# Group statistics in three steps between units, and a first look one block ahead, in a four-layer vision kernel

## The chip, the cores and the metric

The kernel runs on one core of one Trainium2 chip. The time is the device time of one execution in microseconds, as the median of several runs of the same program. The core has five engines, each with an instruction queue of its own: TensorE (PE in the profile, and PEld for its weight loads), VectorE (DVE), ScalarE (ACT), GpSimd (POOL) and SyncE (SP), which here issues most of the data transfers. They wait for one another through semaphores.

## The reference

The input is a batch of 4 images of 56 x 56 positions with 256 channels, in float32. Four residual layers follow one another, each behind a group normalisation without weights:

```python
def _gn(v, G=32, eps=1e-5):
    g = v.reshape(B_, H_, W_, G, C_ // G)
    m = jnp.mean(g, axis=(1, 2, 4), keepdims=True)
    s = jnp.var(g, axis=(1, 2, 4), keepdims=True)
    return ((g - m) / jnp.sqrt(s + eps)).reshape(v.shape)

x = x + L0(_gn(x))   # 7x7 neighbourhood attention, 8 heads, zero padding
x = x + L1(_gn(x))   # all 3136 tokens of an image against each other
x = x + L2(_gn(x))   # 7x7 neighbourhood attention in two halves of the heads, dilation 1 and 2
x = x + L3(_gn(x))   # 7x7 windows shifted by 3, 8 heads, relative position bias
```

Layers 0, 2 and 3 project to queries, keys and values, take softmax(q k + bias) v in the neighbourhood or window, and project the result. Layer 1 normalises each token to unit length, forms exp(5(A - max A)) of A = xn W_adj xn without its diagonal, scales its rows to sum 1, and passes rowsum * (xW + b) - A xW through a layer norm and a leaky ReLU. What matters here is that the mean and the variance of a group of 8 channels run over the whole image: nothing of an image can be normalised in a layer before the last part of that image has left the layer before it.

## The kernel before

`direct_blocks` holds all four layers, one after the other, each over the images 0 to 3. Between layers an image lies in DRAM as channels by tokens. On chip the 256 channels are two halves (`CC` = 2) of 128 partitions.

**Statistics.** `add_stats(l, b, i, x)` (L888) takes `bn_stats` of part i of image b as soon as that part of the input of layer l is on chip: for layer 0 from loads of their own (`first_look`, L1096), for layers 1 to 3 from the output of the layer before (L1220, L1413, L1599). `group_stats(l, b, pm)` (L894) is called when the image is first to be normalised. It puts out, in one go,

- two `bn_aggr` on DVE, which make mean and variance of each channel (`mv`, L901);
- a 128x2 matmul with the matrix `group`, which averages over the 8 channels of a group (L902), and its copy to `gst` (L903);
- three DVE operations on 128x2, which make (channel mean - group mean)^2 + variance (`dv`, L905 to L907);
- a second matmul with `group` over `dv` (L908), eps added on DVE (L909), and the power -0.5 on GpSimd (L910), with a second GpSimd operation that records the numbers (L912).

`normalise` (L914) then applies (x - mean) * scale to a half of a tile on DVE (L915, result `xn`). Both small matmuls take a PSUM buffer with the tag "m" (`ps_m`), of which there are two in layers 0, 2 and 3 and one in layer 1. The same two buffers take every projection: `project` (L917, matmul L921; keys, queries, output) and `value_rows` (L932, matmul L938; values), so that a third projection in a row waits until the first is taken out of PSUM. Keys and queries are taken out by ScalarE, values and the output projection of layers 0 and 2 by DVE.

**Units and steps.** Layers 0 and 2 work on a stream of pairs of tiles (`attend_pairs`, L1006): per pair the scores (PE, L1019), a bias (DVE, L1026) and two exponentials (ACT, L1027 and L1029), two multiplications by table or mask on GpSimd (L1030, L1039), and the products with the values (PE, L1048). TensorE runs the scores of a pair, then `w["fill"]`, then the products of the pair before, so that what lies in the fill covers the time of the exponentials. A unit is 7 rows of an image in layer 0 (8 units per image, 4 pairs each) and 14 rows in layer 2 (4 per image, 8 pairs each). The steps of a unit (projections of a later block, `prepare`, the output projection of the unit before, the building of a table for a later layer) stand in one list, and `spread` (L1068) divides that list evenly by its length over the unit's pairs. Layer 3 does the same by half rows of windows (`attend_quads`, L957), with its list written out for each.

**Layer 0.** Unit r takes `steps` from the rows of projections, puts `project_out(r - 1)` in the middle, and in the first four units of an image loads two parts each of the next image under the tag "xs" (three buffers) and takes their first look; the fourth unit ends with `group_stats(0, b + 1)`. **Layer 1** has the units (image, tile, range of tiles); `tokens(b, c)` normalises 512 tokens, makes their norms (`sq`, L1294; L1299) and projects them, and calls `group_stats(1, b)` for c = 0 (L1287). The accumulation of the products is on DVE (`acc`, L1359). **Layers 2 and 3** call `group_stats` in `prepare`, for the first part of an image (L1473, L1722), about one unit ahead of its use.

In layers 0 to 2 the order of instructions on each engine is set by a scheduler that goes by the order of the program and by priorities; in layer 3 it is the order of the program (`manual_schedule`).

Of the kernel before, what the change touches and what calls it, by code (L numbers as in the profile page):

```python
# [24 lines left out]
FP = mybir.dt.float32  # L25
# [6 lines left out]
NIMG = 4  # L32
# [799 lines left out]
def direct_blocks(ctx: ExitStack, tc: tile.TileContext, d: dict, watch):  # L832
# [38 lines left out]
    def psum_tile(tag, bufs, banks=1):  # L871
        shape = [P, 512] if banks == 1 else [P, banks, 512]
        return ps.tile(shape, FP, tag=tag, name="ps_" + tag, bufs=bufs)

    def ps_m():
        return psum_tile("m", 2)

    def weight(pool, name, n):
        w = pool.tile([P, CC, n], FP, name="w_" + name)
# [3 lines left out]

    parts_of = [NCH, NB0, NCH, 2 * NSB]
    raw = [[const.tile([P, CC, n, 6], FP, name=f"st{l}_{b}") for b in range(NIMG)] for l, n in enumerate(parts_of)]
    stats = {}

    def add_stats(l, b, i, x):  # L888

        if l < 4:  # L890
            for h in range(CC):
                nc.vector.bn_stats(out=raw[l][b][:, h, i, :], in_=x[:, h, :])

    def group_stats(l, b, pm):  # L894

        st = raw[l][b]
        mv = const.tile([P, CC, 2], FP, name=f"mv{l}_{b}")
        gst = stats[l, b] = const.tile([P, CC, 2], FP, name=f"gst{l}_{b}")
        dv = const.tile([P, CC], FP, name=f"dv{l}_{b}")
        for h in range(CC):  # L900
            nc.vector.bn_aggr(out=mv[:, h, :], in_=st[:, h].rearrange("p a b -> p (a b)"))  # L901
        nc.tensor.matmul(pm[:, :CC], lhsT=group, rhs=mv[:, :, 0], start=True, stop=True)  # L902
        nc.vector.tensor_copy(gst[:, :, 0], pm[:, :CC])  # L903

        nc.vector.tensor_tensor(dv, mv[:, :, 0], gst[:, :, 0], ALU.subtract)  # L905
        nc.vector.tensor_tensor(dv, dv, dv, ALU.mult)
        nc.vector.tensor_tensor(dv, dv, mv[:, :, 1], ALU.add)  # L907
        nc.tensor.matmul(pm[:, CC:2 * CC], lhsT=group, rhs=dv, start=True, stop=True)  # L908
        nc.vector.tensor_scalar_add(dv, pm[:, CC:2 * CC], GN_EPS)  # L909
        nc.gpsimd.tensor_tensor(gst[:, :, 1], dv, mhalf, ALU.pow)  # L910
        w = watch[1][:, :2 * CC].rearrange("p (h a) -> p h a", h=CC)
        nc.gpsimd.tensor_tensor(w, w, gst, ALU.add)  # L912

    def normalise(dst, src, gst, h):  # L914
        nc.vector.tensor_scalar(dst, src, gst[:, h, 0:1], gst[:, h, 1:2], ALU.subtract, ALU.mult)  # L915
# [171 lines left out]
    def layer0(big, pool):  # L1087
# [2 lines left out]

        def load(r, held=xs, tag="x"):
            b, g = divmod(r, NCH)
            held[r] = pool.tile([P, CC, CH], FP, tag=tag, name="x0", bufs=3)
            nc.sync.dma_start(out=held[r], in_=tokens_of(0, b, g * CH, CH))

        def first_look(r):  # L1096
# [3 lines left out]
        for r in (3, 4, 5, 6, 0, 1, 2):  # L1100
# [2 lines left out]
                add_stats(0, 0, r, xs[r])  # L1103
            else:
                first_look(r)
        group_stats(0, 0, ps_m())
        wv, wk, wq = (weight(big, n, C) for n in ("wv0", "wk0", "wq0"))
        late_loads()
        wo = weight(big, "wo0", C)
# [10 lines left out]
        def prepare(r):  # L1120
            xn = xns[r] = pool.tile([P, CC, CH], FP, tag="xn", name="xn0")
            x = xs.pop(r)
            for h in range(CC):
                normalise(xn[:, h, :], x[:, h, :], stats[0, r // NCH], h)
            if 3 < r + 2 < NIMG * NCH:
                load(r + 2)

# [96 lines left out]
        def stream():  # L1224
            n = NIMG * NCH
            rows = []
            for c in range(2, n):
                rows += lazily(project_rows, c, 6)
                rows.append(lambda c=c: prepare(c + 1) if c + 1 < n else None)
            gone = 0  # L1230
            for r in range(NIMG * NB0):
                b, g = divmod(r, NB0)
                to = min(len(rows), (7 * (7 * r + 12)) // 8)
                steps, gone = rows[gone:to], to
                if r:
                    at = len(steps) // 2
                    steps[at:at] = project_out(r - 1)
                if b + 1 < NIMG and g < 4:
                    for i in range((b + 1) * NCH + 2 * g, (b + 1) * NCH + min(2 * g + 2, NCH)):
                        load(i, looks, "xs")  # L1240
                        steps.append(lambda i=i: first_look(i))
                    if g == 3:
                        steps.append(lambda b=b: group_stats(0, b + 1, ps_m()))
                if r:
                    steps += table[:3]
                    del table[:3]
                attns[r] = pool.tile([P, CC, BT], FP, tag="attn", name="attn0")
                yield from spread([pair(r, t) for t in range(NTC)], steps)

# [18 lines left out]
    def layer1(big, pool):  # L1268
        NB = -(-T // P)
        real = lambda i: min(P, T - i * P)  # L1270
        ps_a = lambda: psum_tile("m", 1)
        w_aff = weight(big, "waff", C)
        xnT = big.tile([P, CC, NB * P], FP, name="xnT")
        xw = big.tile([P, NB, C + 1], FP, name="xw")
# [7 lines left out]
        def tokens(b, c):  # L1282

            tiles = range(4 * c, min(4 * c + 4, NB))
            n = sum(real(t) for t in tiles)
            if c == 0:
                group_stats(1, b, ps_a())  # L1287
            x = pool.tile([P, CC, 512], FP, tag="x", name="x1")
            nc.sync.dma_start(out=x[:, :, :n], in_=tokens_of(1, b, 4 * c * P, n))
            x1 = pool.tile([P, CC, 512], FP, tag="xn", name="xn1")  # L1290
            sq = pool.tile([P, CC, 512], FP, tag="sq", name="sq")
            for h in range(CC):
                normalise(x1[:, h, :n], x[:, h, :n], stats[1, b], h)
            nc.scalar.activation(sq[:, :, :n], x1[:, :, :n], AF.Square)  # L1294
            k = real(tiles[0])
            pm = ps_a()
# [127 lines left out]
        for k, w in enumerate(units):  # L1424
            b, j, first, last = w
            while waiting and waiting[0][0] <= done:
                waiting.pop(0)[1]()
            if j == 0:
                c = first // 4 + 2 if b == 0 else NC4 - 1 if first == 0 else NC4
                if c < NC4:  # L1430
                    tokens(b, c)
            if first == j:
                residual(b, j * P // CH)
                residual(b, j * P // CH + 1)
                if j % 4 == 2 and j >= 6 and b + 1 < NIMG:
# [14 lines left out]


    def layer2(big, pool):
        (types1, w1), (types2, w2) = window_types(S), window_types(G2)
        w_qkv, w_p = weight(big, "wqkv2", 3 * C), weight(big, "wp2", C)
        bias = big.tile([P, 4, w1 + w2], FP, name="bias2")
# [13 lines left out]

        def prepare(i):  # L1470
            b, c = divmod(i, 2 * NSB)
            if c == 0:
                group_stats(2, b, ps_m())  # L1473
            x = xs.pop(i)
            if i + 1 < NIMG * 2 * NSB:
                load(i + 1)
            xn = xns[i] = pool.tile([P, CC, WC2], FP, tag="xn", name="xn2")
            for h in range(CC):
                normalise(xn[:, h, :], x[:, h, :], stats[2, b], h)

        def project_rows(i):

# [120 lines left out]
        def stream():  # L1603
            n = NIMG * NSB
            for r in range(n):
                steps = []
                for i in (2 * r + 3, 2 * r + 4):
                    if i < 2 * n:
                        steps += lazily(project_rows, i, 6)
                    if i + 1 < 2 * n:  # L1610
                        steps.append(lambda i=i: prepare(i + 1))
                if r:
                    at = max(1, len(steps) // 4)
                    steps = steps or [no_step]
                    steps[at:at] = project_out(r - 1)
                attns[r] = pool.tile([P, CC, 2 * WC2], FP, tag="attn", name="attn2")
                yield from spread([pair(r, m, i) for i in range(4) for m in range(2)], steps)

# [73 lines left out]
    def layer3(big, pool):  # L1692
# [25 lines left out]
            transfer(3, r, xs[r], 0)  # L1718

        def prepare(r):  # L1720
            if r % 8 == 0:
                group_stats(3, r // 8, ps_m())  # L1722
            x = xs.pop(r)
            if r + 1 < NIMG * 8:
                load(r + 1)
            xn = xns[r] = pool.tile([P, CC, WC], FP, tag="xn", name="xn3")
            for h in range(CC):
                for w, xv in parts(xn[:, h, :], x[:, h, :]):
                    normalise(w, xv, stats[3, r // 8], h)

        def project_rows(r):
            xn = xns.pop(r)
# [59 lines left out]
        def stream():  # L1792
            n = NIMG * 8
            for r in range(n):
                attns[r] = pool.tile([P, CC, WC], FP, tag="attn", name="attn3", bufs=3)
                rows = lazily(project_rows, r + 1, 6) if r + 1 < n else []
                out = project_out(r - 2) if r > 1 else []
                for hq in range(CC):
                    steps = out[hq:hq + 1] + rows[3 * hq:3 * hq + 3]
                    if hq and r + 2 < n:  # L1800
                        steps.append(lambda r=r: prepare(r + 2))
                    w = quad(r, hq)
                    w["fill"] = lambda steps=steps: [f() for f in steps]
                    yield w
# [121 lines left out]
```

## Time and profile before

| | before |
|---|---|
| time, median of 3 runs | 4215.47 us (4213.47 to 4218.94) |
| span of the profiled execution | 4208.6 us |
| layer 0 / 1 / 2 / 3, from the trace | 0-807 / 807-2903 / 2903-3624 / 3624-4208 us |
| busy: TensorE, its weight loads | 3983.2, 2790.2 us |
| busy: DVE, ACT, POOL | 2375.0, 1348.8, 1739.3 us |
| sets of group statistics | 16 (4 layers x 4 images), two small matmuls each |

In the profile a busy figure counts the time in which at least one instruction of that engine was under way. Idle time is put down to the instruction that ended it ("waited for"). An entry such as "128x2 f32 x16" gives partitions, elements and count. Some rows carry the line of a helper: L921 is every projection, whichever layer it is in. The granted clock (PEclk) is the share of TensorE's full clock that the chip allowed in that stretch.

### The profile page before, as it was taken

Reading aid. Unit: us, or ns where it says so; the run is one execution under the profiler, and the core shown is the slowest. Engines: PE = TensorE matmul, PEld = TensorE weight load, DVE = VectorE, ACT = ScalarE, POOL = GpSimd, SP = SyncE. Lnnn points to the kernel's source line nnn. Section 1 sums busy time; section 2 is a strip of 40 time slices with the busy share of each in tenths; the row PEclk is TensorE's granted clock in tenths of the full one; section 3 lists DMA queues with packets and bytes.
Section 4 is the critical chain, followed back from the end, with each engine's and each line's share of the span. In section 5 each row is a group of like instructions: output and inputs, shape, how many; then the busy total and the mean of one; then the engine's idle time right before and its main releaser. Section 6 shows DMA issues by size and latency. Waiting matters only on the chain.

```text
span 4208.6 us, 92416 instructions
## 1 busy us (share of the span) xinstructions
PE 3983.2 (95%) x39191; PEld 2790.2 (66%) x39191; DVE 2375.0 (56%) x4437; ACT 1348.8 (32%) x2850; POOL 1739.3 (41%) x1883
## 2 busy tenths in 40 slices
PE   7899999799999999999999999996999999799998
PEld 4566666577777677776777677774666666566665
DVE  6777777533445333453434533344677878566665
ACT  3345545321211112211112111111545555334333
POOL 2466667511124111241112411123766767444444
PEclk9899999899999999999999999998999999899999
DMA  7343333300000000010000000003343433322222
GB/s 254 94 124 118 117 110 107 100 16 9 24 14 28 19 10 24 15 37 10 14 19 24 18 9 9 10 18 119 108 124 116 126 112 117 104 71 71 71 71 64
DMA packets 239793, 275.88 MB, mean 66 GB/s; under 512 B 22150, under 2 KB 231720, under 8 KB 238888
## 3 DMA queue, kind: packets, MB, share of 16 engines
q1 hardware_dynamic: 239082, 269.80, 20.9%
q8 instruction: 310, 5.08, 0.5%
q14 instruction: 113, 0.93, 0.1%
q10 hardware_dynamic: 288, 0.08, 0.0%
HBM read 190.29 MB, written 79.53 MB: 64 GB/s over the span
## 4 chain that ended last, share of the span: by engine, by line
PE 81%; DVE 8%; POOL 5%; issue 2%; DMA 2%; ACT 1%; SPq 0%; DVEq 0%; POOLq 0%; ACTq 0%
PE ps_m L921 17%; PE ps_o L1363 13%; PE ps_v L1355 11%; PE ps_s L1335 11%; PE ps_m L938 8%; PE ps_o L1048 6%; PE ps_s L1019 5%; PE ps_t L1350 3%; PE ps_o L988 2%; POOL b L1039 1%; PE ps_s L973 1%; PE ps_m L1309 1%; PE ps_m L1299 1%; DMA x<-x 1%; POOL rstd L1393 1%
## 5 line engine op out<-in xcount | busy, mean ns | idle before, releaser
L1359 DVE TENSOR_TENSOR acc<-acc,ps_v 128x257 f32<-128x257 f32 x1104 | 459.0, 420 | 677.2 <-PE ps_v L1355 673.0
L1338 ACT ACTIVATE e<-ps_s 128x512 f32<-128x512 f32 (+3 forms) x364 | 200.7, 551 | 1418.3 <-PE ps_s L1335 1418.0
L1355 PE MATMUL ps_v<-xw,e 128*128 128x257 f32 x2400 | 639.9, 384 | 13.6 <-DVE acc L1359 13.6
L1363 PE MATMUL ps_o<-xw,at 128*128 128x257 f32 x2400 | 642.6, 390 | 0.3
L1335 PE MATMUL ps_s<-xnT,xd 128*128 128x512 f32 (+3 forms) x1456 | 631.1, 550 | 0.0
L1363 PEld LDWEIGHTS ps_o<-xw,at 128*128 128x128 f32 x2400 | 436.7, 190 | 128.6 <-ACT at L930 70.7
L1039 POOL TENSOR_TENSOR b<-e 126x336 f32<-126x336 f32 (+5 forms) x512 | 501.2, 1001 | 11.2 <-ACT e L1027 3.1
L1355 PEld LDWEIGHTS ps_v<-xw,e 128*128 128x128 f32 x2400 | 423.1, 191 | 93.5 <-DVE acc L1359 33.8
L1331 POOL TENSOR_SCALAR xd<-xnT,vec 128x128 f32<-128x128 f32 x200 | 121.9, 621 | 812.4 <-PE ps_s L1335 807.1
L921 PE MATMUL ps_m<-xn,w_wqkv 128*128 128x392 f32 x1024 | 370.8, 502 | 16.0 <-DVE xn L915 15.8
L1335 PEld LDWEIGHTS ps_s<-xnT,xd 128*128 128x128 f32 x1456 | 264.1, 190 | 141.2 <-issue 117.2
L1030 POOL TENSOR_TENSOR e<-e,m0t 126x672 f32<-126x672 f32 (+3 forms) x128 | 238.7, 1865 | 270.7 <-ACT e L1029 270.7
L1030 POOL TENSOR_TENSOR e<-e,bias 119x784 f32<-119x784 f32 (+5 forms) x128 | 239.8, 1873 | 223.0 <-ACT e L1029 222.9
L951 ACT ACTIVATE no<-rs 128x168 f32<-128x168 f32 (+2 forms) x256 | 93.8, 367 | 625.4 <-DVE rs L1562 288.9
L921 PEld LDWEIGHTS ps_m<-xn,w_wqkv 128*128 128x128 f32 x1024 | 188.6, 191 | 150.3 <-ACT pr L1785 17.2
L938 PE MATMUL ps_m<-w_wqkv,xn 128*98 128x256 f32 x1024 | 246.8, 390 | 19.9 <-DVE xn L915 19.9
L1048 PEld LDWEIGHTS ps_o<-e,vp 124*32 124x32 f32 (+3 forms) x8192 | 174.0, 110 | 135.9 <-issue 76.8
L915 DVE TENSOR_SCALAR xn<-x,gst 128x28 f32<-128x28 f32 (+4 forms) x368 | 202.2, 604 | 95.9 <-PE ps_m L921 50.5
L1350 PEld LDWEIGHTS ps_t<-ident,e 128*128 128x128 f32 x1200 | 152.2, 142 | 143.0 <-issue 136.4
L1048 PE MATMUL ps_o<-e,vp 124*32 124x112 f32 (+3 forms) x8192 | 235.4, 252 | 4.0 <-POOL e L1030 3.4
L1562 DVE RECIPROCAL rs<-ps_o 128x196 f32<-128x196 f32 (+2 forms) x128 | 176.4, 1378 | 99.6 <-PE ps_o L1048 97.0
L940 DVE TENSOR_TENSOR v<-ps_m,bc 98x512 f32<-98x512 f32 (+1 forms) x184 | 125.4, 687 | 188.2 <-PE ps_m L938 111.4
(149 smaller groups left out, 6260.3 us busy)
## 6 DMA issues: line engine op xcount, KB each, us to landing
x<-xr SPq DMA_DIRECT2D x64, 392.0 KB
x<-in_x SPq DMA_DIRECT2D x53, 448.0 KB
x<-x SPq DMA_DIRECT2D x60, 392.0 KB
xr<-x SPq DMA_DIRECT2D x60, 392.0 KB
vd<-v SPq DMA_DIRECT2D x28, 448.0 KB
xr<-in_x SPq DMA_DIRECT2D x32, 392.0 KB
xr<-x SPq DMA_DIRECT2D x28, 448.0 KB
x<-xr SPq DMA_DIRECT2D x28, 448.0 KB
```

The lines of the kernel that those rows point to most:

```text
L915: nc.vector.tensor_scalar(dst, src, gst[:, h, 0:1], gst[:, h, 1:2], ALU.subtract, ALU.mult)
L921: nc.tensor.matmul(pm[:, :n], lhsT=w[:, h, col:col + P], rhs=rhs(h), start=(h == 0), stop=(h == CC - 1))
L938: nc.tensor.matmul(pm[:n, j * C:(j + 1) * C], lhsT=xn[:, h, k * n:(k + 1) * n], rhs=w[:, h, :], start=(h == 0), stop=(h == CC - 1))
L1019: nc.tensor.matmul(s[j // 2][:nk, j % 2, (2 * i + u) * nq:(2 * i + u + 1) * nq], lhsT=k(j, u), rhs=q(j), start=True, stop=True)
L1030: nc.gpsimd.tensor_tensor(parts(ev), parts(ev), w["emask"], ALU.mult)
L1039: nc.gpsimd.tensor_tensor(w["b"][a][:nk, :, :2 * nq].rearrange("p h (i c) -> p h i c", i=2), ev[:, :, :, 0, :], ev[:, :, :, 1, :], ALU.add)
L1048: nc.tensor.matmul(w["o"](k, i)[j * HD:(j + 1) * HD], lhsT=ones[:nk, :HD] if k else v(j, u), rhs=w["b"][j // 2][:nk, j % 2, i * nq:(i + 1) ...
L1335: nc.tensor.matmul(s[:, :n], lhsT=xd[j][:, h, :], rhs=xnT[:, h, first * P:last * P], start=(h == 0), stop=(h == CC - 1))
L1350: nc.tensor.transpose(pt[:, col(i)], e[:, col(i)], ident)
L1355: nc.tensor.matmul(pv[:, :C + 1], lhsT=e[:, col(i)], rhs=xw[:, j, :], start=True, stop=True)
L1359: nc.vector.tensor_tensor(acc[:, i, :], acc[:, i, :], pv[:, :C + 1], ALU.add)
L1363: nc.tensor.matmul(out[j][:, :C + 1], lhsT=e[:, col(i)] if i == j else at[:, col(i)], rhs=xw[:, i, :], start=(i == j), stop=(i == NB - 1))
```

## The change

The statistics of an image are no longer computed where they are first needed but as soon as the last part of the image is known, and in three steps that can stand apart: `channels` (the two `bn_aggr`), `mean` (the first matmul to `dv`) and `scale` (the second matmul to the power). `add_stats` counts the parts, and the last one puts the three steps into `pending`. `step_stats` does one of them, if there is one, and stands in the lists of steps: in layer 0 three times in the first unit of an image and in the last four, in layer 1 at every fourth unit, in layer 2 three times in every unit from the second on, in layer 3 at the end of each half row. `known(l, b)` takes the place of `stats[l, b]` and does whatever is left. So that steps which are left over may run in the next layer, `ps_m` takes its number of buffers from `m_bufs`, and each layer sets it as it was.

In layer 0 the parts for the first look are loaded one unit ahead of the look (`look_at`), into four buffers instead of three, and the looks come first in a unit's list. `project_out` goes in last, so that its place in the middle is reckoned in the longer list.

```diff
     def add_stats(l, b, i, x):
         if l < 4:
             for h in range(CC):
                 nc.vector.bn_stats(out=raw[l][b][:, h, i, :], in_=x[:, h, :])
-    def group_stats(l, b, pm):
+            seen_parts[l, b] = seen_parts.get((l, b), 0) + 1
+            if seen_parts[l, b] == parts_of[l]:
+                pending.extend(group_stats(l, b))
+
+    def group_stats(l, b):
...
+        def channels():
...
+        def mean():
+            pm = ps_m()
...
+        def scale():
+            pm = ps_m()
...
+            stats[l, b] = gst
+        return [channels, mean, scale]
+
+    def step_stats():
+        if pending:
+            pending.pop(0)()
+
+    def known(l, b):
+        while (l, b) not in stats:
+            pending.pop(0)()
+        return stats[l, b]
...
-            held[r] = pool.tile([P, CC, CH], FP, tag=tag, name="x0", bufs=3)
+            held[r] = pool.tile([P, CC, CH], FP, tag=tag, name="x0", bufs=3 if tag == "x" else 4)
...
+            look_at = {}
+            for b in range(NIMG - 1):
+                for i in range(NCH):
+                    look_at.setdefault(NB0 * b + min(i // 2 + (b == 0), 3), []).append((b + 1) * NCH + i)
             for r in range(NIMG * NB0):
...
-                if r:
-                    at = len(steps) // 2
-                    steps[at:at] = project_out(r - 1)
-                if b + 1 < NIMG and g < 4:
-                    for i in range((b + 1) * NCH + 2 * g, (b + 1) * NCH + min(2 * g + 2, NCH)):
-                        load(i, looks, "xs")
-                        steps.append(lambda i=i: first_look(i))
-                    if g == 3:
-                        steps.append(lambda b=b: group_stats(0, b + 1, ps_m()))
+                steps += [lambda i=i: first_look(i) for i in sorted(looks)]
+                steps.append(lambda r=r: [load(i, looks, "xs") for i in look_at.get(r + 1, [])])
+                for i in range(3 if g > 3 or g == 0 else 0):
+                    steps.insert(2 * i, step_stats)
                 if r:
                     steps += table[:3]
                     del table[:3]
+                    at = (len(steps) + 1) // 2
+                    steps[at:at] = project_out(r - 1)
...
         def tokens(b, c):
-            if c == 0:
-                group_stats(1, b, ps_a())
...
         for k, w in enumerate(units):
+            if k % 4 == 2:
+                step_stats()
...
@@ layer 2, prepare and stream @@
-            if c == 0:
-                group_stats(2, b, ps_m())
...
                     steps[at:at] = project_out(r - 1)
+                    for _ in range(3):
+                        at = min(at + 5, len(steps))
+                        steps.insert(at, step_stats)
...
@@ layer 3, prepare and stream @@
-            if r % 8 == 0:
-                group_stats(3, r // 8, ps_m())
...
                         steps.append(lambda r=r: prepare(r + 2))
+                    steps.append(step_stats)
```

Every normalisation reads `known(l, b)` instead of `stats[l, b]`.

More of the change, by code (lines that the diff above doesn't have):

```diff
@@ L873, in psum_tile @@
         return ps.tile(shape, FP, tag=tag, name="ps_" + tag, bufs=bufs)
+    m_bufs = 2
     def ps_m():
-        return psum_tile("m", 2)
+        return psum_tile("m", m_bufs)
     def weight(pool, name, n):
@@ L885, in direct_blocks @@
     raw = [[const.tile([P, CC, n, 6], FP, name=f"st{l}_{b}") for b in range(NIMG)] for l, n in enumerate(parts_of)]
-    stats = {}
+    stats, pending = {}, []
+    seen_parts = {}
     def add_stats(l, b, i, x):
@@ L892, in add_stats @@
                 nc.vector.bn_stats(out=raw[l][b][:, h, i, :], in_=x[:, h, :])
-    def group_stats(l, b, pm):
+            seen_parts[l, b] = seen_parts.get((l, b), 0) + 1
+            if seen_parts[l, b] == parts_of[l]:
+                pending.extend(group_stats(l, b))
+    def group_stats(l, b):
         st = raw[l][b]
         mv = const.tile([P, CC, 2], FP, name=f"mv{l}_{b}")
-        gst = stats[l, b] = const.tile([P, CC, 2], FP, name=f"gst{l}_{b}")
+        gst = const.tile([P, CC, 2], FP, name=f"gst{l}_{b}")
@@ L899, in group_stats @@
         dv = const.tile([P, CC], FP, name=f"dv{l}_{b}")
[L900 to L912, printed above, removed]
+        def channels():
+            for h in range(CC):
+                nc.vector.bn_aggr(out=mv[:, h, :], in_=st[:, h].rearrange("p a b -> p (a b)"))
+        def mean():
+            pm = ps_m()
+            nc.tensor.matmul(pm[:, :CC], lhsT=group, rhs=mv[:, :, 0], start=True, stop=True)
+            nc.vector.tensor_copy(gst[:, :, 0], pm[:, :CC])
+            nc.vector.tensor_tensor(dv, mv[:, :, 0], gst[:, :, 0], ALU.subtract)
+            nc.vector.tensor_tensor(dv, dv, dv, ALU.mult)
+            nc.vector.tensor_tensor(dv, dv, mv[:, :, 1], ALU.add)
@@ new lines, in scale @@
+        def scale():
+            pm = ps_m()
+            nc.tensor.matmul(pm[:, :CC], lhsT=group, rhs=dv, start=True, stop=True)
+            nc.vector.tensor_scalar_add(dv, pm[:, :CC], GN_EPS)
+            nc.gpsimd.tensor_tensor(gst[:, :, 1], dv, mhalf, ALU.pow)
+            w = watch[1][:, :2 * CC].rearrange("p (h a) -> p h a", h=CC)
+            nc.gpsimd.tensor_tensor(w, w, gst, ALU.add)
+            stats[l, b] = gst
[3 more added lines that the diff above has]
+            pending.pop(0)()
@@ L1105, in layer0 @@
                 first_look(r)
-        group_stats(0, 0, ps_m())
+        known(0, 0)
         wv, wk, wq = (weight(big, n, C) for n in ("wv0", "wk0", "wq0"))
@@ L1123, in prepare @@
             for h in range(CC):
-                normalise(xn[:, h, :], x[:, h, :], stats[0, r // NCH], h)
+                normalise(xn[:, h, :], x[:, h, :], known(0, r // NCH), h)
             if 3 < r + 2 < NIMG * NCH:
@@ L1270, in layer1 @@
         real = lambda i: min(P, T - i * P)
-        ps_a = lambda: psum_tile("m", 1)
+        nonlocal m_bufs
+        m_bufs, ps_a = 1, ps_m
         w_aff = weight(big, "waff", C)
@@ L1292, in tokens @@
             for h in range(CC):
-                normalise(x1[:, h, :n], x[:, h, :n], stats[1, b], h)
+                normalise(x1[:, h, :n], x[:, h, :n], known(1, b), h)
             nc.scalar.activation(sq[:, :, :n], x1[:, :, :n], AF.Square)
@@ L1452, in layer2 @@
     def layer2(big, pool):
+        nonlocal m_bufs
+        m_bufs = 2
         (types1, w1), (types2, w2) = window_types(S), window_types(G2)
@@ L1478, in prepare @@
             for h in range(CC):
-                normalise(xn[:, h, :], x[:, h, :], stats[2, b], h)
+                normalise(xn[:, h, :], x[:, h, :], known(2, b), h)
         def project_rows(i):
@@ L1728, in prepare @@
                 for w, xv in parts(xn[:, h, :], x[:, h, :]):
-                    normalise(w, xv, stats[3, r // 8], h)
+                    normalise(w, xv, known(3, r // 8), h)
         def project_rows(r):
```

## The prediction

> **What bounds the kernel now.** I read the page's busy times and slices first, then the waits of TensorE, then the timeline of one place where group statistics are computed, then equal stretches of time beside each other for their cost.
>
> ```profile
> span 4208.6 us, 92416 instructions
> PE 3983.2 (95%) x39191; PEld 2790.2 (66%) x39191; DVE 2375.0 (56%) x4437; ACT 1348.8 (32%) x2850; POOL 1739.3 (41%) x1883
> PEclk9899999899999999999999999998999999899999
> ```
>
> TensorE is busy 95% of the span and nothing else is over 56%. So the time is TensorE's work, plus its idle 225 us (4208.6 - 3983.2), plus what it loses where its granted clock is below 1. An edit that leaves the work alone, as this one does, can only win from the last two. The waits of TensorE, as "who waited <- for what: us in total, times, longest":
>
> ```profile
> PE ps_m L908 <- DVE dv L907: 28.7, 13, 3.8
> ...
> PE ps_m L902 <- DVE mv L901: 18.6, 4, 14.5
> ...
> PE ps_m L921 <- ACT no L951: 14.2, 7, 2.7
> PE ps_v L1355 <- DVE acc L1359: 13.6, 43, 1.6
> PE ps_m L921 <- DVE attn L1194: 10.7, 6, 2.7
> PE ps_m L921 <- ACT kE L1145: 10.6, 6, 3.8
> ```
>
> L902 and L908 are the two matmuls of the statistics, L921 a projection. The 14.5 us of L902 is the program's start. The rest of L908 is what the change aims at. One such place, in layer 2 (columns: start, duration, engine, line, operation; the bracket is the idle time before):
>
> ```profile
> 3053.69 0.28 PE L902 MATMUL ps_m<-mv,group 128*128 128x2 f32 x2
> 3053.90 0.86 PE L1048 MATMUL ps_o<-e,vp 119*32 119x98 f32 x26
> 3053.97 2.09 POOL L1030 TENSOR_TENSOR e<-e,bias 124x896 f32<-124x896 f32 x1 [2.54 <-ACT e L1029]
> ...
> 3054.20 1.87 DVE L905 TENSOR_TENSOR dv<-mv,gst 128x2 f32<-128x2 f32 x1
> ...
> 3056.02 2.21 POOL L1039 TENSOR_TENSOR b<-e 124x448 f32<-124x448 f32 x2
> 3056.11 1.05 DVE L906 TENSOR_TENSOR dv<-dv 128x2 f32<-128x2 f32 x1
> 3057.20 1.05 DVE L907 TENSOR_TENSOR dv<-dv,mv 128x2 f32<-128x2 f32 x1
> ...
> 3058.30 0.38 PE L908 MATMUL ps_m<-dv,group 128*128 128x2 f32 x2 [3.54 <-DVE dv L907]
> ```
>
> Three operations on 128x2 take 1.87, 1.05 and 1.05 us; each ends as one of GpSimd's ends, and where GpSimd is still they take 0.10 to 0.16. TensorE has 26 attention matmuls to do meanwhile (0.86 us) and then sits for 3.54 us behind the second matmul, although the attention matmuls queued after it need nothing from it. The idle time is not all: the same attention work before, after and behind the gap (columns: window, sum; busy PE, PEld, DVE, ACT, POOL; granted clock, DMA share, GB/s):
>
> ```profile
> 3013.00:3019.00 6.00, 6.00 (x109) 4.64 (x100) 5.97 (x7) 2.50 (x6) 4.42 (x4) 1.00 0.57 161
> 3059.50:3068.40 8.90, 8.90 (x106) 6.54 (x100) 6.89 (x9) 2.03 (x4) 3.94 (x5) 0.67 0.42 121
> 3104.00:3110.00 6.00, 6.00 (x116) 4.65 (x114) 5.47 (x7) 2.41 (x5) 5.51 (x5) 1.00 0.58 163
> ```
>
> The clock falls to 0.67 on average, and 106 matmul records take 8.9 us where 109 take 6.0: the gap costs almost as much again afterwards.
>
> [...]clock records at 0.5 follow the statistics gaps and last 3.41 us or twice that.[...] So what decides a wait is how much of TensorE's own work stands between the two small matmuls.[...]
>
> **The change, part by part.** Every engine keeps its instructions; only the order moves. I take the cost of an episode from equal stretches: what a unit with statistics takes over its neighbours, less 0.55 us for the four small matmul records that stay (0.28 + 0.38, less what overlaps).
>
> Layer 3: a half row takes 8.25 us (distance of successive ones in the timeline); the three with statistics, at 3759, 3895 and 4032, take 4.55, 4.55 and 6.41 more, although the idle gaps there are only 1.35 at L902 and 0.83 at L908; the rest is half clock. Sum 15.5, less 3 x 0.55 = **13.9 us**. In the changed order these sets are computed in layer 2, with their two matmuls two pairs (some 10 us) apart, so no wait is left; I take 14.
>
> Layer 2: a unit takes 41.3 us; with statistics 49.0, 47.3 and 48.9, sum 21.3, less 1.6 = **19.7 us**. These sets move into layer 1, which has one episode less of its own. Against it: the three statistics steps that are inserted into a unit's list, nearly all of them empty, shift all later steps over the pairs, in every unit from the second on. A projection needs one of two PSUM buffers of tag m, so a third in one pair must wait until the first is emptied. Before, 13 units have such a pair, "output, key, key", whose first buffer DVE empties in about 0.6 us; weight loads wait on DVE's L1597 there for 4.1 us in all, 0.3 each. After, that pair is gone, and 13 units have "key, output, output" in one pair and "key, key, query" in another, whose first buffer ScalarE empties. In a pair of before (3085) the key projection starts at 3084.98 and the second projection ends at 3087.9; ScalarE empties the keys, behind two exponentials of 0.80 and 0.86 us, from 3087.77 to 3088.89. A third one would so have waited 1.0 us there. ScalarE's place varies by some 0.6 us: between 0.4 and 1.0, and I take 0.7. 26 x 0.7 = 18 us given back, less the 4 of the pair that went: 14. Bounds: 26 x 0.4 - 4 = 6 and, by the waits of layer 0 on L1145 without the longest, (10.6 - 3.8)/5 = 1.36, 26 x 1.36 - 4 = 31. Layer 2: 19.7 - 14 = **+6**.
>
> Layer 0: three episodes cost 5.7, 7.6 and 7.0 over neighbouring units, 20.3 less 1.6 = 18.7. Afterwards the first matmul and the second lie a pair apart in four places, with attention (1.26), scores (1.13) and a value projection (1.6 to 1.9) between them: 4.0 to 4.3 us of work against 4.1 us of the three DVE operations at their slowest; that hides them but for some 0.2. In two further places (pairs 12.3 and 20.3) only 15 of the attention matmuls lie between, and I leave 1 us in each (0.7 to 2.4, as GpSimd's multiplication is over or not). So 16. project_out moves later in the unit. Before, it waits 2.05 and 2.56 us in two units per image, behind a DVE that normalises (L915 up to 2.4 us beside GpSimd), and four half-clock windows of 3.41 us follow (259.6, 283.5, 464.4, 645.4). I take half of these away: 4 images x 2.1 = 8.5. But three projections in a row become more frequent ("key, query, output", "two outputs, value"): three or four more per image at 0.59 to 1.0 us, -2 x 4 = -8. Together 16 + 8.5 - 8, **+16**. The looks of the next image one block ahead: in both orders the scheduler has already put nearly all looks into the first 125 us, where DVE waits for loads (14.8 us in nine waits at L892, hidden but for some of TensorE's start): nothing, give or take 5 us.
>
> Layer 1: three starts of an image cost 1.58 us each at L1355, and the last two a half-clock window of 6.83 us, 3.4 lost; with some small losses around, 1.6 + 4.4 + 4.4 = 10.4. The operations that cause it are GpSimd's power (0.26 us waited) and two normalisations (1.41) in front of DVE's accumulation; the statistics are then known beforehand, but the normalisations stay, at a time when DVE is just as full. I take **+8**. The layer's other sets are popped between units, where TensorE's waits are short.
>
> The starts of layers 1, 2 and 3 (5.89, 19.9 and 15.8 us of waiting) wait for loads behind the last stores; the statistics are over before the load lands, and the order of the queue there is unchanged: **0**.
>
> Sum: 14 + 6 + 16 + 8 = 44 us. 4215.5 - 44 = 4171.5; I say **4172**.
>
> **Rivals.** A: the new waits for buffers are as long as those of layer 0 (1.36 each, 31 us net): layer 2 becomes -11, the sum 14 - 11 + 16 + 8 = 27, the time 4189. For it: the same pattern is in before's layer 0; against it: ScalarE has less queued in layer 2. B: the third projection finds its buffer, in layers 0 and 2: layer 2 wins 20 + 4, layer 0 16 + 8, layer 1 10, layer 3 14, sum 72, time 4143. For it: ScalarE is busy only 32%, and a few tenths of delay elsewhere would hide the emptying; against it: the 1.0 us read above. C, slower: as A, and each such wait is followed by a half-clock window of 3.41 us, 1.7 lost: 26 x (1.36 + 1.7) - 4 = 76, so layer 2 is 20 - 76 = -56, the sum 14 - 56 + 16 + 8 = -18, the time 4233. For it: gaps of 1.35 us in layer 3 and 1.58 in layer 1 did bring half clock; against it: the single waits of about 1 and 0.6 us on L921 in layer 0 did not.
>
> **How the numbers follow.** The forecast has 0.55, A 0.2, B 0.15, C 0.1. The range takes A whole, the bounds of the forecast (buffer waits 6 to 31 us, layer 0 from 5 to 25), and ends at B: 4143 to 4204. Slower by over 0.2% (above 4224) is C and a little of A with a bad start: 0.08; within 0.2%, 4207 to 4224, what lies between A and C: 0.05; faster 0.87.
>
> **What would show it.** Right: L908 leaves the waits or stays under 5 us in all; the half-clock windows after 3058, 3232, 3403, 3761, 3898 and 4034 are gone; layer 3 is 14 us shorter; L921 waits on ScalarE's keys in layer 2, some 26 times, 10 to 35 us, and the units without statistics are about 1 us longer than 41.3. Wrong: units of layer 2 still at 41.3 (B), or a clock below 1 in them all (C); L908 still waiting 2 us and more, or layer 0 longer than before, would break the sum at its largest terms.

## The result: slower, and the profile after

| | before | after |
|---|---|---|
| time, median of 4 runs each | 4216.19 us (4213.47 to 4218.94) | 4232.24 us (4228.68 to 4235.25) |
| ratio after / before | | 1.0038, 95% interval 1.0020 to 1.0055 |
| layer 0, from the trace | 806.1 us | 818.0 us |
| layer 1 | 2094.4 | 2083.9 |
| layer 2 | 723.2 | 758.2 |
| layer 3 | 584.8 | 573.4 |
| span of the profiled execution | 4208.6 | 4233.4 |

A layer ends here with the last matmul of its output (layer 2: with the start of TensorE's long wait for layer 3's first load; before, 2.3 us of layer 3's first statistics lie in front of that wait and are counted with layer 2). The profiled executions differ by 24.9 us, the medians by 16; the first figure is shared out among the layers, from unrounded times: +11.9, -10.6, +34.9, -11.4. The forecast, 4172 us, was wrong in sign: layers 1 and 3 win about what it said, layers 0 and 2 do the opposite.

The page of the changed kernel:

```profile
span 4233.4 us, 92399 instructions
PE 3982.2 (94%) x39191; PEld 2782.0 (66%) x39191; DVE 2384.8 (56%) x4437; ACT 1346.7 (32%) x2850; POOL 1736.1 (41%) x1883
```

TensorE does the same work and is idle 251 us instead of 225. Its waits, for the whole span (line numbers have moved: L946 is the projection, L913 and L922 the two small matmuls):

```profile
PE ps_m L946 <- ACT kE L1525: 35.1, 26, 3.0
PE ps_m L946 <- DVE v L965: 24.3, 11, 4.8
...
PE ps_m L946 <- DVE attn L1219: 16.9, 7, 3.6
...
PE ps_m L922 <- DVE dv L918: 4.3, 3, 1.7
```

The wait that the change aims at is gone, 28.7 to 4.3 us. In its place stand 26 waits for the buffer of layer 2's keys, and waits for DVE to take the values out of PSUM. The first are easiest to see in units of layer 2 that have no statistics at all, before and after (window, sum; busy PE, PEld, DVE, ACT, POOL; clock, DMA share, GB/s):

```profile
3161.10:3202.80 41.70, 41.70 (x724) 29.27 (x720) 32.48 (x42) 22.44 (x52) 30.03 (x25) 1.00 0.43 127
```

```profile
3176.30:3220.60 44.30, 42.33 (x729) 29.17 (x724) 32.45 (x42) 22.29 (x53) 31.09 (x27) 1.00 0.40 118
```

Same work, same full clock, 2.6 us longer: TensorE never stopped in this unit before, and now stands for 2.0 us, in two waits of about 1.

A unit of layer 2 that has statistics, after the change, in the timeline:

```profile
3021.57 1.77 DVE L916 TENSOR_TENSOR dv<-mv,gst 128x2 f32<-128x2 f32 x1
...
3023.37 0.80 DVE L917 TENSOR_TENSOR dv<-dv 128x2 f32<-128x2 f32 x1
3024.20 0.80 DVE L918 TENSOR_TENSOR dv<-dv,mv 128x2 f32<-128x2 f32 x1
3024.93 0.68 DVE L965 TENSOR_TENSOR v<-ps_m,bc 98x512 f32<-98x512 f32 x1
3025.53 1.54 DVE L1589 RECIPROCAL rs<-ps_o 128x224 f32<-128x224 f32 x1
...
3025.66 1.58 PE L946 MATMUL ps_m<-xn,w_wqkv 128*128 128x392 f32 x4 [0.88 <-DVE v L965]
...
3030.21 2.98 PE L946 MATMUL ps_m<-xn,w_wqkv 128*128 128x392 f32 x4 [2.96 <-ACT kE L1525]
```

The second small matmul is a pair further on and no longer waits. But the three operations on 128x2 still take 3.4 us of DVE, and what stands behind them in DVE's queue comes late: first the values' evacuation (so TensorE waits 0.88 us for the buffer), then the reciprocal, the next pair's bias and exponentials, and with them the emptying of the keys (2.96 us instead of the usual 1.1). That the 2.96 us come from the three operations is read from this order; no run has this list with shorter operations. Half clock follows (stretches in which the granted clock is 0.5): 3.41 to 6.83 us at 3029, 3169, 3350 and 3531, one for each set, and no others from the layer's first scores to its last unit.

### The profile page after: what moved, and what is told of

Read it like the earlier page. It is cut to its first block, busy times and chain, and to the rows that moved or that the text cites. A ratio compares the mean times of both kernels' runs of the same rounds, so it can differ in the third digit from the quotient of the medians.

```text
span 4233.4 us, 92399 instructions
## 1 busy us (share of the span) xinstructions
PE 3982.2 (94%) x39191; PEld 2782.0 (66%) x39191; DVE 2384.8 (56%) x4437; ACT 1346.7 (32%) x2850; POOL 1736.1 (41%) x1883
## 4 chain that ended last, share of the span: by engine, by line
PE 76%; DVE 13%; POOL 4%; issue 3%; ACT 2%; DMA 2%; SPq 0%; DVEq 0%; POOLq 0%; ACTq 0%
PE ps_m L946 15%; PE ps_o L1388 13%; PE ps_v L1380 11%; PE ps_s L1360 11%; PE ps_m L963 6%; PE ps_o L1073 5%; PE ps_s L1044 3%; PE ps_t L1375 3%; PE ps_o L1013 2%; DVE e L1051 2%; DVE rs L1589 2%; PE ps_s L998 1%; DVE rs L1217 1%; PE ps_m L1324 1%; DVE xn L940 1%
## 5 line engine op out<-in xcount | busy, mean ns | idle before, releaser
L946 PE MATMUL ps_m<-xn,w_wqkv 128*128 128x392 f32 x1024 | 380.2, 510 | 45.1 <-ACT kE L1525 21.8
L946 PEld LDWEIGHTS ps_m<-xn,w_wqkv 128*128 128x128 f32 x1024 | 187.7, 192 | 183.1 <-ACT kE L1525 31.6
L963 PE MATMUL ps_m<-w_wqkv,xn 128*98 128x256 f32 x1024 | 244.8, 385 | 23.4 <-DVE xn L940 22.7
L1052 ACT ACTIVATE e<-e 126x672 f32<-126x672 f32 (+5 forms) x256 | 219.5, 858 | 35.7 <-DVE e L1051 17.2
```

Of the source, the lines that this page charges most:

```text
L946: nc.tensor.matmul(pm[:, :n], lhsT=w[:, h, col:col + P], rhs=rhs(h), start=(h == 0), stop=(h == CC - 1))
L963: nc.tensor.matmul(pm[:n, j * C:(j + 1) * C], lhsT=xn[:, h, k * n:(k + 1) * n], rhs=w[:, h, :], start=(h == 0), stop=(h == CC - 1))
```

## The experiments

Theory 1: **the grouping of projections**. The new lists of steps put more projections into one pair than there are PSUM buffers of tag m (layer 2), and the output projection behind a late DVE (layer 0). Theory 2: **the DVE chain**. The three operations, held up by GpSimd, block DVE for 2 to 4 us wherever they stand, so that moving them moves the wait to whoever is behind them on DVE. Each predicts something else for the runs below, each timed against the kernel before on the same chip. The runs e1 to e4, e5 to e8 and e9 were on three chips, on which the kernel before took 4217.3, 4216.8 and 4210.5 us; between these groups the ratios compare better than the times.

| run | median us | ratio to before (95%) | layers 0 / 1 / 2 / 3, us |
|---|---|---|---|
| e1_l2_list | 4192.2 | 0.9939 (0.9922 to 0.9957) | 821.8 / 2087.0 / 715.7 / 571.7 |
| e2_before_shift | 4251.7 | 1.0083 (1.0068 to 1.0099) | 811.9 / 2097.9 / 763.4 / 587.1 |
| e3_l0_old | 4224.7 | 1.0018 (1.0011 to 1.0026) | 810.5 / 2084.3 / 757.8 / 574.0 |
| e4_before_one_port | 4197.9 | 0.9956 (0.9940 to 0.9971) | 807.0 / 2087.5 / 718.3 / 582.3 |
| e5_list_port | 4172.2 | 0.9896 (0.9881 to 0.9911) | 800.4 / 2083.9 / 713.3 / 571.3 |
| e6_list_out | 4188.1 | 0.9932 (0.9914 to 0.9950) | 821.8 / 2085.6 / 716.9 / 571.6 |
| e7_l0_old_port | 4175.5 | 0.9902 (0.9888 to 0.9917) | 803.9 / 2084.4 / 715.8 / 571.0 |
| e8_l0_old_list | 4183.6 | 0.9915 (0.9902 to 0.9928) | 811.3 / 2087.6 / 715.7 / 571.2 |
| e9_out_g7 | 4160.9 | 0.9878 (0.9862 to 0.9895) | 787.6 / 2087.1 / 717.8 / 572.9 |

Two runs with the same code in layer 0 (before and e2, after and e1) differ by 4 to 6 us there, most of it in the first four units, which wait for loads. Differences of that size in the layer's total are not read; single units are compared instead. (A unit's length is the time from its first scores to those of the next. It can vary too: unit 23 takes 21.8 us before and 25.0 in e2, with the same code and the same wait of 2.1 us.)

**e1_l2_list.** Changed kernel, layer 2:

```diff
-                    for _ in range(3):
-                        at = min(at + 5, len(steps))
-                        steps.insert(at, step_stats)
+                    for k in range(3):
+                        at = min(at + 4, len(steps) - 1)
+                        steps[at] = lambda f=steps[at]: (f(), step_stats())
```

> The changed kernel, but in layer 2 a statistics step is tied to a step that stands in the list anyway instead of being a list entry of its own, so spread() divides the list over the pairs as it did before the change. Theory 1 (the grouping of projections): the 26 waits on ScalarE's keys (35 us) go, layer 2 falls from 758 to about 715 us, the time from 4232 to about 4190. Theory 2 (the DVE chain: the three operations on 128x2 block DVE beside GpSimd wherever they stand): only the four waits of 0.9 us on the values and the 3.0 us waits that follow them belong to it, the waits on the keys stay at over 20 us, the time stays above 4220.

Layer 2 falls by 42 us and the time by 40. TensorE's longest waits in layer 2 of this kernel, after that for the layer's first load:

```profile
PE ps_m L963 <- DVE v L965: 7.5, 4, 1.9
```

No wait on the keys is left. Theory 1 holds for layer 2. The four units with statistics (1, 4, 8 and 12) still take 44.8, 44.6, 46.1 and 46.2 us against 41.7, 42.0, 40.9 and 40.9 before: 16 us for four sets. e5 comes back to these.

**e2_before_shift.** Kernel before, layer 2:

```diff
                     steps[at:at] = project_out(r - 1)
+                    for _ in range(3):
+                        at = min(at + 5, len(steps))
+                        steps.insert(at, no_step)
```

> The kernel before, with three steps that do nothing put into the list of layer 2 where the change has its statistics steps; nothing else differs. Theory 1: 26 waits on ScalarE's keys of about 1.2 us appear, layer 2 grows by 30 to 38 us, the time is about 4250. Theory 2: without moved statistics there is no such cost, the time stays within 5 us of 4216.

Three list entries that emit no instruction cost 34 us. The wait appears with them:

```profile
PE ps_m L908 <- DVE dv L907: 28.7, 13, 3.8
PE ps_m L921 <- ACT kE L1498: 27.4, 26, 1.2
```

26 waits, 1.05 us each, and the old wait beside them unchanged. The empty entries alone, since they change how the even division falls, cost as much as the whole net loss of layer 2 (34.9 us).

**e3_l0_old and e8_l0_old_list.** The changed kernel, and e1, with layer 0's list as before:

```diff
-                steps += [lambda i=i: first_look(i) for i in sorted(looks)]
...
-                    steps.insert(2 * i, step_stats)
+                if r:
+                    at = len(steps) // 2
+                    steps[at:at] = project_out(r - 1)
...
+                        steps.append(lambda b=b: known(0, b + 1))
```

> The changed kernel, but layer 0 has its list as before (looks, place of project_out, statistics of the next image at once in the fourth unit). Layers 1 to 3 as changed. Theory 1: layer 0 goes back from 818 to 807 us, the time from 4232 to 4221, since the waits of 3.6 us on DVE's attn and the waits on DVE's v are made by the new list. Theory 2: the statistics cost the same in both lists, so only what the first units won (7 us) is lost: layer 0 at 818 to 825, the time 4232 to 4239.

> As e7_l0_old_port without the one-port operations: layer 0 as in e3_l0_old (810), layer 1 2085, layer 2 as in e1_l2_list (715), layer 3 572, sum 4182 and a time near 4183. Against e1 (4192) it gives the cost of the new layer 0 list: 9 us by theory 1, below 3 by theory 2.

The old list is 7.5 us faster in the one (4232.2 to 4224.7) and 8.6 in the other (4192.2 to 4183.6): near theory 1's number, but this comparison does not say whether the place of project_out or the statistics in the list do it. e5, e7 and e9 take these two apart.

**e4_before_one_port.** Kernel before; TensorE's order is the same but for the second small matmul, which stands a few matmuls further on or back, and for a few matmuls beside it (in unit 3 of layer 0, and the norms' matmuls L1299 at three starts of an image in layer 1):

```diff
-        nc.vector.tensor_tensor(dv, mv[:, :, 0], gst[:, :, 0], ALU.subtract)
-        nc.vector.tensor_tensor(dv, dv, dv, ALU.mult)
-        nc.vector.tensor_tensor(dv, dv, mv[:, :, 1], ALU.add)
+        nc.vector.tensor_tensor(dv, mv[:, :, 0], pm[:, :CC], ALU.subtract)
+        for h in range(CC):
+            nc.vector.tensor_scalar(dv[:, h:h + 1], dv[:, h:h + 1], dv[:, h:h + 1], mv[:, h, 1:2], ALU.mult, ALU.add)
```

> The kernel before, in its order, but the three operations that make dv take at most one tensor from SBUF: the subtraction reads the group mean from PSUM, and square and sum are two tensor_scalar operations with scalars per partition (same numbers, same count). Theory 2: they take about 0.16 us each instead of 1 to 2, the waits at the second small matmul fall from 28.7 to under 8 us, with the half clock behind them the time falls by 30 to 45, to about 4178. If the durations are not GpSimd's doing, they stay at 1 to 2 us and the time at 4216.

The tile dv, durations in ns as min/median/max, of the kernel before and then of this one:

```profile
L905 DVE TENSOR_TENSOR dv<-mv,gst x16: 96/160/1977, 15.3 to 4034.0; 128x2 f32<-128x2 f32 x16
L906 DVE TENSOR_TENSOR dv<-dv x16: 95/160/1996, 15.5 to 4034.2; 128x2 f32<-128x2 f32 x16
L907 DVE TENSOR_TENSOR dv<-dv,mv x16: 160/352/1053, 15.7 to 4034.4; 128x2 f32<-128x2 f32 x16
```

```profile
L907 DVE TENSOR_SCALAR dv<-dv,mv x32: 203/266/274, 14.3 to 4021.0; 128x1 f32<-128x1 f32 x32
...
L905 DVE TENSOR_TENSOR dv<-mv,ps_m x16: 135/146/148, 14.1 to 4020.6; 128x2 f32<-128x2 f32 x16
```

With one tensor from SBUF the spread up to 2 us is gone. In the kernel before, the 27 of these 48 operations beside which GpSimd is still take 0.10 to 0.16 us, the 21 beside which it works 0.29 to 2.00. In the subtraction nothing changed but the place of one input, and at the place below it takes 0.15 us while GpSimd's 2.10 us operation runs, where before it took 1.87 beside one of 2.09. For the subtraction, then, it is the second input from SBUF that made it long beside GpSimd; the other two also became another operation, and no run tells the two changes apart. The waits at the second small matmul fall from 28.7 to 8.8 us. But the time falls by 19 us only, half of what was expected. The timeline of the same place that the prediction showed (then 3.54 us of waiting at the second small matmul) says why:

```profile
3048.01 2.10 POOL L1030 TENSOR_TENSOR e<-e,bias 124x896 f32<-124x896 f32 x1 [2.54 <-ACT e L1029]
...
3048.13 0.15 DVE L905 TENSOR_TENSOR dv<-mv,ps_m 128x2 f32<-128x2 f32 x1
...
3048.82 0.38 PE L908 MATMUL ps_m<-dv,group 128*128 128x2 f32 x2
...
3050.07 2.21 POOL L1039 TENSOR_TENSOR b<-e 124x448 f32<-124x448 f32 x2
3052.25 0.70 POOL L910 TENSOR_TENSOR gst<-dv,mhalf 128x2 f32<-128x2 f32 x1
3052.99 0.88 DVE L915 TENSOR_SCALAR xn<-x,gst 128x392 f32<-128x392 f32 x2 [3.59 <-POOL gst L910]
...
3053.62 0.72 PE L938 MATMUL ps_m<-w_wqkv,xn 128*98 128x256 f32 x1 [2.77 <-DVE xn L915]
```

The second matmul comes at once, and the next link of the chain takes its place: the power stands in GpSimd's queue behind 2.2 us of multiplication, the normalisation behind the power, and TensorE waits 2.77 us for that. The three units of layer 2 with statistics fall only from 49.2, 47.6 and 49.2 us to 48.1, 47.0 and 47.0. So short operations alone do not hide a set here. What an earlier start is worth beside them is seen in layer 3: 582.3 us in this run, 571 to 574 in all runs with the changed order.

**e5_list_port.** e1 with these operations.

> The changed kernel with the layer 2 list of e1_l2_list and the one-port operations of e4_before_one_port. Theory 2 for what is left in layer 0 (the three operations, still 1 to 2 us beside GpSimd, hold up the evacuation of the values and the second matmul): in layer 0 the waits on DVE's v at units 12, 20 and 28 (2.3 each) and on dv (1.7 each) go, with half clock some 10 us; layer 0 from 820 to about 810, the time from 4192 to about 4180. Theory 1 (only the grouping counts): layer 0 and the time as in e1, 4192.

4172.2, 20 us below e1. Layer 0's units 12, 20 and 28, which hold two sets, two and one, fall from 29.8, 30.6 and 27.5 to 24.3, 24.3 and 22.8 us; their waits for DVE's v and dv (2.3 to 2.4 and 1.7 us each) are gone. Theory 2 holds for what is left in layer 0: in the changed order it was the DVE chain that made the statistics units as long as before.

In layer 2 it does not. Units 1, 4, 8 and 12 take 44.8, 44.5, 44.5 and 46.3 us, hardly less than in e1, and TensorE still waits 1.8 to 2.0 us in each for the values:

```profile
2998.02 1.97 PE L963 MATMUL ps_m<-w_wqkv,xn 128*98 128x256 f32 x8
...
2999.83 0.28 PE L913 MATMUL ps_m<-mv,group 128*128 128x2 f32 x2
...
3002.05 0.68 DVE L965 TENSOR_TENSOR v<-ps_m,bc 98x512 f32<-98x512 f32 x1
...
3002.78 1.97 PE L963 MATMUL ps_m<-w_wqkv,xn 128*98 128x256 f32 x8 [1.79 <-DVE v L965]
```

The first small matmul (L913) takes one of the two buffers between two value projections, so that the second projection has to wait until DVE has emptied the buffer of the first. (In the kernel before the two small matmuls of a set share one buffer; in the changed kernel each asks for one.) This is read from the timeline; no run takes the small matmuls out of these buffers.

**e7_l0_old_port.** e8 with these operations.

> The layer 0 list of before, layer 1 and 3 as changed, the layer 2 list of e1_l2_list, and the one-port operations: what should be the best of all by both theories. Layer 0 807 (e4) , layer 1 2084, layer 2 713, layer 3 572: about 4176 and a time near 4177. If the one-port operations win nothing once the statistics stand apart, it equals e8.

8 us below e8, and not better than e5 (the intervals of the ratios overlap): once the operations are short, layer 0's new list is no longer the slower one. That fits the view that the 8 us between the lists in e3 and e8 are the price of the three more sets (those of layer 1) that the new list brings into layer 0.

**e6_list_out and e9_out_g7.** The place of project_out. In the changed kernel TensorE waits 3.58 us for it in units 7, 15 and 23:

```profile
246.97 2.09 POOL L1055 TENSOR_TENSOR e<-e,m0t 95x896 f32<-95x896 f32 x1 [0.98 <-ACT e L1054]
246.97 3.58 DVE L940 TENSOR_SCALAR xn<-x,gst 128x448 f32<-128x448 f32 x2
...
252.47 0.39 DVE L1219 TENSOR_TENSOR attn<-ps_o,rs 128x224 f32<-128x224 f32 x1
...
252.92 1.25 PE L946 MATMUL ps_m<-attn,w_wo 128*128 128x392 f32 x3 [3.58 <-DVE attn L1219]
```

Two normalisations take 3.58 us, with GpSimd at work beside them, and delay the last attention of the unit before, which the output projection needs. e6 is e1 with project_out in the middle of the rows before looks and statistics steps are added; e9 is e5 with that only where g == 7:

```diff
                 steps, gone = rows[gone:to], to
+                if g == 7:
+                    at = len(steps) // 2
+                    steps[at:at] = project_out(r - 1)
...
-                    at = (len(steps) + 1) // 2
-                    steps[at:at] = project_out(r - 1)
+                    if g != 7:
+                        at = (len(steps) + 1) // 2
+                        steps[at:at] = project_out(r - 1)
```

> The changed kernel with the layer 2 list of e1_l2_list, and in layer 0 project_out put into the middle of the rows before looks and statistics steps are added, as before the change. Theory 1: the three waits of 3.6 us on DVE's attn come from project_out's new place in the list; they and their half clock go, layer 0 from 820 to about 812, the time from 4192 to about 4184. Theory 2: the waits belong to DVE's normalisations beside GpSimd (3.6 us for two), and follow the output projection to another pair: layer 0 within 4 us of 820.

> e5_list_port with project_out at its old place in the list, but only in the last unit of each image (g == 7) in layer 0; TensorE's order differs in these places alone. Theory 1 (place in the list): the three waits of 3.6 us on DVE's attn at units 7, 15 and 23 go and these units fall from 26.1, 26.7 and 25.2 to about 21.8 us, 12 us in all; the time goes from 4172 to about 4160. Theory 2 (the normalisations beside GpSimd hold up whatever follows them): the wait moves to the values' projection or the scores of the same units, which stay above 25 us; the time stays at 4172.

In e6 units 7, 15 and 23 fall by 6.1, 4.4 and 6.0 us to 21.8, but its first four units take 8 us more and others some tenths, so that the time (4188) is not clearly different from e1's: inconclusive. e9 changes TensorE's order in layer 0 in three places only, and units 7, 15 and 23 fall from 26.1, 26.7 and 25.2 to 21.8, 21.8 and 22.7 us. The wait in layer 0 from 170 us on was 16.9 us (7 times, 3.6 the longest) after the change, and in e9

```profile
PE ps_m L946 <- DVE attn L1219: 6.1, 4, 2.6
```

In these units TensorE now waits 1.45 us for DVE before the scores, instead of the 3.58. e9 is the change with three of its side effects taken out. Its time, 4160.9 us, is the lowest, but the kernel before was faster on that chip too: the ratios of e9 and e5, 0.9878 and 0.9896, have overlapping intervals. The 11.7 us are shown for the three units; in the time they are not separated from the noise.

## Why the prediction was wrong

**Right: layers 1 and 3.** Forecast 8 and 14 us, measured 10.6 and 11.4 (13.8 in layer 3, counted from the last output of layer 2), and again in e1 and e5 to e9 (layer 1 at 2084 to 2088, layer 3 at 571 to 573). The mechanism was right too. L908's wait fell to 4.3 as foretold, and the half clock after it in layer 3 (3.41, 3.41 and 6.83 us at 3761, 3898 and 4034) went; in layer 1 the two stretches of half clock of 6.83 us, at 1584 and 2103, went, and the waits for DVE's accumulation fell from 13.6 to 8.6 us.

**Wrong, first step: "26 x 0.7 = 18 us given back" in layer 2, 14 net.** The mechanism was named and the 26 places are there; the size was short by half. The waits are 1.05 us each where no statistics interfere (e2). And these waits cost more than their idle time: the units without statistics are 2.5 to 2.8 us longer for two waits of 2.0 to 2.2 us together, 1.3 to 1.4 each, so 26 x 1.35 = 35 us, near what e2 costs. The pair "output, key, key" that went gave nothing to set against it: its weight loads waited, but TensorE was busy in all of the 41.70 us of the unit shown. The wait of 1.0 read from the place at 3085 was the right one; to go down to 0.7 for ScalarE's varying place was not supported by any row.

**Wrong, second step: "so no wait is left" for the sets that come into layer 2, and "that hides them" in layer 0.** The prediction asked only whether TensorE's second matmul would wait for dv, and put the sets at nothing in their new places. It did not ask what is queued behind the three operations on DVE, nor what a small matmul takes from the projections. Layer 2's own sets did leave units 2, 6 and 10, and 20.9 us went with them, near the 19.7. But units 1, 4, 8 and 12, with one set of layer 2 and three of layer 3, are 9.1, 7.1, 8.2 and 8.2 us longer than before, sum 32.5, less 4 x 2.8 of the grouping: 21 us for four sets, where nothing was forecast. In layer 0, units 12 and 20, now with two sets each, take 29.8 and 29.4 us after 29.4 and 28.9, and unit 28 has a set it did not have, 28.4 after 21.9: 7 us lost, where 16 were to be won. The statistics were moved, and their price moved with them. For layer 0 e5 shows that it was the DVE chain: with the operations short, 16.6 us go from these three units. For layer 2 it stays open how the 21 us divide: 16 are left in e1, without the grouping, and 15 in e5, with short operations as well, where the buffer that the small matmul takes is the wait that is seen.

**Wrong, third step: "I take half of these away: 4 images x 2.1 = 8.5" for project_out.** That half did go: in units 8, 16 and 24 its wait of 2.59 to 2.69 us is gone, and they are 2.9, 2.9 and 4.1 us shorter. But in units 7, 15 and 23 the later place brings it behind the two normalisations, a wait of 3.58 us where it was 2.07 to 2.08, and they are 3.3, 6.0 and 4.3 us longer: 13.6 lost against 9.9 won. Each wait stands in three places, and not in four as the sum took it. The prediction had no term for the loss; in e9 the old place is worth 11.7 us in these units.

The rival that came near was C, 4233: slower by the buffer waits. That its number fits is chance: it needed half clock after each of these waits, and none of the 22 waits of about 1.05 us in the changed kernel's layer 2 is followed by any. And it kept the 16 us that layer 0 was to win, where 11.9 were lost. The loss came from about twice the forecast's cost for a wait, from the statistics' price coming back, and from the place of project_out.

What stays open: layer 0's first four units vary by some 4 to 8 us among kernels that hardly differ there, and what the first look a block ahead is worth was not tried by itself. Of layer 0's loss, units 5, 6, 13, 14, 21 and 22, which are 7.6 us longer in all, were not explained, nor was the prediction's -8 for three projections in a row tested.

## What to carry to other kernels

A list that is divided evenly by its length is a schedule: an entry that does nothing moves everything behind it. Tie optional work to entries that exist, and count what each pair then asks of its shared buffers. When a wait is to be hidden by moving a chain of small operations, ask for each engine that the chain passes what is queued behind it there, ask what buffers the moved operations take, and make the operations short as well. Here earlier alone, with the list repaired, gave 25 us (e1), short alone 19 (e4), and both 45 (e5).

## What the runs showed of the hardware

In the kernel before, the 48 operations of DVE on 128x2 that make dv, with two inputs from SBUF, take 0.10 to 0.16 us in the 27 cases in which no operation of GpSimd overlaps them, and 0.29 to 2.00 in the 21 in which one does. In e4 the subtraction, with one input from PSUM, takes 0.14 to 0.15, and the tensor_scalar on 128x1 with scalars per partition 0.20 to 0.27.

Two stops of TensorE, of 0.93 and 1.05 us, came with 0.5 us more than their idle time at full clock: from its first scores to those of the next unit, unit 5 of layer 2 (the one shown above) takes 41.75 us before and 44.26 after, with 720 matmul records both times, and TensorE's busy time rises from 41.75 to 42.28 us. (Ends of matmuls are modelled in the profile, so the sum, 2.5 us for two stops, is surer than its parts.)

How often a stop of TensorE was followed by half clock was counted in the first 14 units of layer 2 in all eleven traces. None of the 78 stops of 0.88 to 1.21 us is followed by it within 3.5 us, 10 of the 23 of 1.76 to 1.97 us are, and all 17 of 2.77 to 3.54 us. (One stop of 2.30 us, in e6, is.) In e1 units 8 and 12, whose stops of 1.95 us are followed by 3.41 us of half clock, take 46.1 and 46.2 us; units 1 and 4, with stops of 1.81 and 1.76 us and none, take 44.8 and 44.6.
